# One core of Trainium2: attention and a mixture of experts in one kernel, with another order at the end of attention and the token lists' one-hots written in pairs

## The chip, the core and the metric

The kernel runs on one core of one Trainium2 chip. The core has five engines, each with its own in-order instruction queue: TensorE (PE; its weight loads are shown apart as PEld), VectorE (DVE), ScalarE (ACT), GpSimd (POOL) and SyncE (SP), which here only issues DMAs. Sixteen DMA engines serve all queues. The metric is the time of one execution on the device, in microseconds (us).

## What is computed

The input x has 8 sequences of 1024 tokens with 256 features. The reference, cut to what matters:

```python
x = x + attn(layernorm(x))        # 16 heads of 16, rotary q and kv, keys are also the values, softmax over 1024 keys
xf = layernorm(x)                 # 8192 rows of 256
x = x + ffn(xf)

def ffn(xf):
    scores = softmax(xf @ gate_w.T)              # 8 experts
    vals, idx = top_k(scores.T, 1024)            # each expert takes its 1024 best tokens
    y = layernorm(xf[idx]) * ln_w + ln_b
    h = gelu(y @ fc1.T + b1)                     # 1024 hidden units
    out = (h @ fc2.T + b2) * vals                # weighted by the score
    return xf.at[idx].add(out)                   # scattered back
```

## The kernel before

**Attention.** A group is four heads of one sequence, so 8 sequences make 32 groups. A group has 16 steps: two halves of 512 queries, and for each half eight tiles of 128 keys. In a step PE makes the scores of one key tile for two pairs of heads (`ps_s`, L587), ACT takes their exponential (`e`, L620), and every second step PE multiplies the two last tiles of `e` with the values (`ps_av`, L639). The products of two steps are copied by ACT (`avp`, L652) and added to `av` by POOL (L654); the very last add of the kernel's attention is on DVE, by the flag `end`. Beside this the row maxima of scores 13 steps ahead are taken (L536 on PE, L543 on DVE); they are over 13 steps before the end.

The order is written out by hand. A loop over steps calls the work of the step and then `run_pieces`, which advances the waiting generators by one piece each: `urgent` ones all, of `ends` the first only. A piece that yields a number waits as many steps; one that yields "x" wants a step where heavy work is let in, "y" one where light work is, and near the end every step lets both in; "d" wants a step that is even. After the loop `finish(urgent)` runs what is left there, and then the two epilogues advance in turn, one piece each, until they are done. Each engine's queue keeps the order in which its instructions were written.

When a half of a group has all its keys, `divide` turns `av` so that tokens lie on partitions (`ps_d`, L665), and divides by the sum of the exponentials (L671, L673) into `ao`. It yields 4, then "y". When the last group of a sequence has a half divided, an `epilogue` for that half of the sequence (512 tokens) is queued. Its pieces, in order:

1. fetch of the residual; 2. transposes of `ao` on PE and copies by ACT (`aoT`, L718); 3. and 4. output product for two token tiles each (`ps_o`, L725) and its add to the residual on DVE (L733); 5. to 8. the mean and variance of one token tile each on DVE (L219, L220), the last also with the reciprocal deviation on POOL (L222, L224), the normalised rows `xf` (L242), a second deviation (`again`, L232 to L236) and the add of `xf` to the residual (L739); 9. transposes of `xf` and copies (`xfT`, L767); 10. gate product (`ps_g`, L773) and its copy `lg` (L781); 11. its transpose (`ps_gt`, L784), maximum, difference `z` and exponential (L787 to L792); 12. sum, reciprocal and scores `sc` (L795 to L799); 13. nothing; 14. transpose of the scores (`ps_sc`, L804), copy `turned` (L806), and four DMAs into `by_expert` (L809).

`lg` and `turned` share one buffer (tag "lg", one of it). In the last sequence the first half's four score DMAs go alternately from the queues of SP and ACT, as the second half's do. Its `xf` and row scaling are on DVE, in earlier sequences on POOL. The write of `out` (L740) is issued in piece 8, the scaling of the rows (`rows`, L750) and their write to `rows_d` (L814) in piece 14 after the score DMAs. `rows_d` holds, for every token, its second normalisation and its eight scores; the experts gather from it. The output rows are what the experts' results are later added to.

**Choice of tokens.** A search over 30 bits finds each expert's threshold (L1009 to L1018): DVE counts the scores of `by_expert` that are not below the candidate, PE sums the counts, DVE sets the next candidate. Then each token's place in its expert's list is computed (L1027 to L1073).

**Token lists.** `token_list(e, LOW)` turns places into a list of token numbers by products of one-hot matrices. A place is split into a low and a high part (L1090, L1091, cast to bf16 at L1093). `high` (L1095) is one where the high part equals the column's number; `ids` holds `high` times the partition's number (L1103) and times the tile's number (L1104); `low` (L1129) is one where the low part equals the column's number, in chunks of 1024 columns. PE multiplies `low` and `ids` (`ps_i`, L1115), and two small DVE instructions make the index (L1142, L1144). In `high`, the second `ids` and `low`, one input is a number repeated over the whole inner row. The first list uses LOW = 64: `high` and `ids` of 1024 columns and four chunks of `low`, all of it before the experts. The other lists use LOW = 128: 512 columns and eight chunks, made in pieces beside the experts; those for experts 3 to 7 beside the second products of experts 1 to 5.

**Experts.** POOL gathers a list's rows by indirect DMA (L1152), PE transposes them (`ps_y`, L1167), DVE scales (`yT`, L1168). Expert 0 has a plain first layer (L1189), the others one with seven products in place of eight (L1230, with sums of weights on POOL at L1208 to L1211, sums of rows on DVE at L1217 to L1220). The second layer (`ps_o`, L1284) is followed by a bias add and a scaling on DVE (L1292, L1293) and an indirect DMA from POOL that adds to `out` (L1294). The next weights are loaded from SP (L959, L961).

Of the kernel before, what the change touches and what calls it, by code (L numbers as in the profile page):

```python
# [10 lines left out]
BF16 = mybir.dt.bfloat16  # L11
# [3 lines left out]
ALU = mybir.AluOpType  # L15
# [4 lines left out]
P = 128  # L20
# [7 lines left out]
def preln_attention_moe_kernel(  # L28
# [18 lines left out]
    nc = tc.nc  # L47
    B, N, D = x.shape
# [49 lines left out]
    with ExitStack() as actx:  # L98
# [531 lines left out]
        def weigh_values(i, half, chunk):  # L630

            b, g = divmod(i, NG)
            pa = ps_m.tile([P, QW], F32, tag="m", name="ps_av")
            for n, (kt, es) in enumerate(chunk):
                for h in range(4):
                    c = VS * (4 * g + h)
                    nc.tensor.matmul(  # L639
                        pa[HS * h : HS * (h + 1), :],  # L640
                        lhsT=v_bufs[b % 2][:, kt, c : c + HS],
                        rhs=es[h // 2][:, h % 2, :],
                        start=(n == 0),
                        stop=(n == len(chunk) - 1),
                    )
            if chunk[0][0] == 0:
                grp[i]["av"] = small.tile([P, QW], F32, tag="av", name="av")
                nc.scalar.copy(grp[i]["av"], pa)
            else:
                av = grp[i]["av"]  # L650
                part = small.tile([P, QW], F32, tag="avp", name="avp", bufs=3)
                nc.scalar.copy(part, pa)  # L652
                end = i == B * NG - 1 and half == 1 and chunk[-1][0] == T - 1
                (nc.vector if end else nc.gpsimd).tensor_tensor(av, av, part, ALU.add)  # L654
                if chunk[-1][0] == T - 1:
                    urgent.append(Task(divide(i, half, av)))

        def divide(i, half, av):

            b, g = divmod(i, NG)  # L660
            yield 4
            yield "y"
            pt = ps_m.tile([P, T2, 4, HS], F32, tag="m", name="ps_d")
            for t in range(T2):
                nc.tensor.transpose(  # L665
                    pt[:, t].rearrange("p h d -> p (h d)"), av[:, t * P : (t + 1) * P], ident
                )
            if b not in outs:
                outs[b] = side.tile([P, T, D], F32, tag="ao", name=f"ao_{b}")
            rden = small.tile([P, T2, 4, 1], F32, tag="rden", name="rden")  # L670
            nc.vector.reciprocal(rden, pt[:, :, :, DH : DH + 1])  # L671
            dst = outs[b][:, T2 * half : T2 * (half + 1), 4 * g * DH : 4 * (g + 1) * DH]
            nc.vector.tensor_tensor(  # L673
                dst.rearrange("p t (h d) -> p t h d", h=4),
                pt[:, :, :, 0:DH],
                rden.to_broadcast([P, T2, 4, DH]),
                ALU.mult,
            )
            finished[(i, half)] = True
# [20 lines left out]
        def residual_ahead(b, hf):  # L700
            xt = residual(b, hf)
            yield 5
            add_bias(xt)

        def epilogue(b, hf):
            ao = outs[b]
            tok = slice(hf * QW, (hf + 1) * QW)
# [32 lines left out]
            out_dma = lambda: nc.sync.dma_start(  # L740
                out[b, tok, :].rearrange("(t p) d -> p t d", p=P), xt
            )
            if last:
                out_dma()

            rows = side.tile([P, T2, ROW], F32, tag="rows", name=f"rows_{b}_{hf}")

# [58 lines left out]
            nc.scalar.copy(turned, ps[0 : T2 * E, 0:P])  # L806
            t0 = b * T + hf * T2
            for t in range(T2):
                (nc.scalar if last and t % 2 else nc.sync).dma_start(  # L809
                    by_expert[t0 // T2 :: NB, t * P : (t + 1) * P], turned[t * E : (t + 1) * E, :]  # L810
                )
            if last:
                rows_scaled()
            nc.sync.dma_start(  # L814
                rows_d[t0 * P : (t0 + T2) * P, :].rearrange("(t p) d -> p t d", p=P), rows
            )

# [166 lines left out]
    nc.gpsimd.iota(turn_i, pattern=[[1, 2], [2, KT]], base=0, channel_multiplier=0)  # L986
    turn = sel.tile([P, 2 * KT], BF16, name="turn")
    nc.gpsimd.tensor_copy(turn, turn_i.rearrange("p a c -> p (a c)"))
    part_i = sel.tile([P, 1], I32, name="part_i")
    nc.gpsimd.iota(part_i, pattern=[[0, 1]], base=0, channel_multiplier=1)  # L990
    part = sel.tile([P, 1], F32, name="part")
# [89 lines left out]
    def token_list(e, LOW, ahead=1):  # L1081
# [7 lines left out]
        halves_i = hot.tile([P, 2, NT], I32, tag="halves_i", name=f"halves_i{e}")  # L1089
        nc.vector.tensor_scalar(halves_i[:, 0], mine, LOW - 1, None, ALU.bitwise_and)  # L1090
        nc.vector.tensor_scalar(halves_i[:, 1], mine, LOW.bit_length() - 1, None, ALU.logical_shift_right)  # L1091
        split = hot.tile([P, 2, NT], BF16, tag="split", name=f"split_{e}")
        nc.vector.tensor_copy(split, halves_i)  # L1093
        high = hot.tile([P, NT, HIGH], BF16, tag=f"high{LOW}", name=f"high_{e}")
        nc.vector.tensor_tensor(  # L1095
            high,
            split[:, 1].unsqueeze(2).to_broadcast([P, NT, HIGH]),
            order.unsqueeze(1).to_broadcast([P, NT, HIGH]),
            ALU.is_equal,
        )  # L1100
        yield
        ids = hot.tile([P, NT, 2, HIGH], BF16, tag=f"ids{LOW}", name=f"ids_{e}")
        nc.vector.tensor_scalar(ids[:, :, 0, :], high, part, None, ALU.mult)  # L1103
        nc.vector.tensor_tensor(  # L1104
            ids[:, :, 1, :],
            high,
            lane[:, 0:NT].unsqueeze(2).to_broadcast([P, NT, HIGH]),
            ALU.mult,
        )
        pi = ps_i.tile([P, 2, KT], F32, tag="pi", name="ps_i")  # L1110
        def summed(c, low):
# [13 lines left out]
        for c in range(NT // CH):  # L1125
# [1 line left out]
            low = hot.tile([P, 1024], BF16, tag="low", name=f"low_{e}_{c}", bufs=4)  # L1127
            low = low.rearrange("p (c l) -> p c l", l=LOW)
            nc.vector.tensor_tensor(  # L1129
                low,  # L1130
                split[:, 0, c * CH : (c + 1) * CH].unsqueeze(2).to_broadcast([P, CH, LOW]),
                lane[:, 0:LOW].unsqueeze(1).to_broadcast([P, CH, LOW]),
                ALU.is_equal,
            )
            lows.append((c, low))
# [289 lines left out]
```

## Time and profile before

| what | us |
|---|---|
| median of three runs | 2227.04 (2224.79 to 2232.28) |
| profiled execution, its own time | 2223.82 |
| span of its instructions | 2222.1 |
| attention, to the last `ps_av` | 1655.7 |
| end of attention, to the first count of the search | 32.5 |
| search and places, to the first write of `by_token` | 50.7 |
| first list, to its index | 10.0 |
| first gather and transposes | 8.1 |
| experts, to the end | 465.0 |

The stretches add up to the span; their borders are read from the timeline, and the rest of the execution's own time, 1.7 us, lies around the span. Over the span PE is busy 92%, DVE 82%, ACT 62% and POOL 58%.

A line of the profile names a source line, an engine, an operation, and what it writes and reads (out<-in); a count and a time follow. "idle before" is the time in which the engine had nothing to run ahead of these instructions, with what ended it. "q" behind an engine means its queue: there it issues a DMA or waits. In the slices a digit is the busy share of one fortieth of the span in tenths; PEclk is the clock that TensorE was granted, in the same way.

### The profile page before, as it was taken

To read this page: it belongs to the slowest core of one execution; us is meant where nothing else is said; L and a number is where in the kernel's file an instruction comes from. 1 tells how busy PE (TensorE), PEld (TensorE's weight loads), DVE (VectorE), ACT (ScalarE), POOL (GpSimd) and SP (SyncE) were. 2 spreads that over 40 slices of the span, in tenths; PEclk is the share of its full clock that TensorE was granted. 3 is DMA by queue.
4 is the path that set the end of the run, shared out by engine and by line. 5 is a ranking of instruction groups with operands and counts; after the bars stand their busy time and mean duration, and the time that the engine had idled before them with its cause. 6 is when DMAs were issued, how large, how long until landed. Compare 5 with 4: busy or idle time off the path is not lost.

```text
span 2222.1 us, 35016 instructions
## 1 busy us (share of the span) xinstructions
PE 2054.7 (92%) x12476; PEld 1095.6 (49%) x12476; DVE 1816.0 (82%) x3443; ACT 1382.3 (62%) x1783; POOL 1292.2 (58%) x1319
## 2 busy tenths in 40 slices
PE   7999999999999999999999999999982599999998
PEld 4444544444444444444444444444441366666665
DVE  8988888998998899889889988989936667777754
ACT  2777777777887787778787777878770012222221
POOL 6667585748476765858494766724242154555542
PEclk8999999999999999999999999999995699999999
DMA  6523624632472355236225722642113033333322
GB/s 178 185 93 122 235 80 157 217 114 78 145 263 81 107 198 195 78 136 238 96 79 174 255 78 69 229 173 78 41 40 134 20 79 70 76 75 77 74 45 24
DMA packets 152702, 271.51 MB, mean 122 GB/s; under 512 B 15056, under 2 KB 67664, under 8 KB 152400
## 3 DMA queue, kind: packets, MB, share of 16 engines
q1 hardware_dynamic: 139056, 250.61, 32.9%
q0 software_dynamic: 12288, 17.05, 4.7%
q8 instruction: 98, 1.61, 0.3%
q10 hardware_dynamic: 1184, 1.62, 0.2%
q14 instruction: 76, 0.62, 0.1%
HBM read 143.93 MB, written 125.04 MB: 121 GB/s over the span
## 4 chain that ended last, share of the span: by engine, by line
PE 69%; DVE 18%; issue 5%; POOL 3%; ACT 2%; DMA 2%; SPq 0%; POOLq 0%; ACTq 0%; DVEq 0%
PE ps_av L639 20%; DVE mx L543 13%; PE ps_x L536 13%; PE ps L1230 8%; PE ps_o L1284 7%; PE ps_s L587 7%; PE ps_p L292 5%; PE ps_t L251 3%; PE ps_o L725 3%; PE ps_h L1189 1%; POOL xf L242 1%; ACT e L620 1%; DVE low L1129 1%; PE ps_d L665 1%; DVE xr L733 1%
## 5 line engine op out<-in xcount | busy, mean ns | idle before, releaser
L543 DVE TENSOR_REDUCE mx<-ps_x 128x1 f32<-128x512 f32 x2048 | 1265.0, 682 | 154.4 <-PE ps_x L536 141.1
L620 ACT ACTIVATE e<-ps_s 128x1024 f32<-128x1024 f32 x1024 | 995.3, 1025 | 87.7 <-PE ps_x L536 35.7
L536 PE MATMUL ps_x<-k,q 64*128 64x512 f32 x2048 | 719.0, 450 | 19.6 <-DVE mx L543 6.6
L587 PE MATMUL ps_s<-q,s 64*128 64x512 f32 x2048 | 622.9, 428 | 10.0 <-ACT e L620 7.1
L536 PEld LDWEIGHTS ps_x<-k,q 64*128 64x128 f32 x2048 | 348.0, 186 | 413.4 <-DVE mx L543 287.9
L639 PE MATMUL ps_av<-e,v 128*32 128x512 f32 x4096 | 492.7, 599 | 7.0 <-DVE mx L543 0.9
L654 POOL TENSOR_TENSOR av<-av,avp 128x512 f32<-128x512 f32 x191 | 243.3, 1274 | 391.7 <-ACT avp L652 375.5
L587 PEld LDWEIGHTS ps_s<-q,s 64*128 64x128 f32 x2048 | 314.3, 185 | 49.0 <-ACT e L620 31.6
L1294 POOL DMA_INDIRECT out<-o,idx x64 | 114.5, 1790 | 215.0 <-DVE o L1293 80.7
L1284 PE MATMUL ps_o<-w,hT 128*128 128x256 f32 x1024 | 230.2, 381 | 0.0
L639 PEld LDWEIGHTS ps_av<-e,v 128*32 128x32 f32 x4096 | 107.4, 109 | 241.6 <-issue 163.8
L1284 PEld LDWEIGHTS ps_o<-w,hT 128*128 128x128 f32 x1024 | 192.1, 190 | 29.0 <-issue 4.8
L652 ACT COPY avp<-ps_av 128x512 f32<-128x512 f32 x192 | 112.6, 587 | 143.8 <-PE ps_av L639 141.3
L1242 ACT COPY mid<-ps 128x512 f32<-128x512 f32 x28 | 16.0, 570 | 203.7 <-PE ps L1230 203.7
L1182 ACT ACTIVATE hT<-mid,b 128x512 f32<-128x512 f32 x112 | 77.8, 718 | 98.9 <-DVE mid L1257 73.8
L292 PE MATMUL ps_p<-wqkv,xnT 128*128 128x512 f32 (+1 forms) x288 | 130.6, 581 | 4.4 <-DVE mx L543 4.1
L1152 POOL DMA_INDIRECT g<-rows_d,idx x64 | 69.9, 1092 | 85.2 <-issue 75.5
L269 POOL TENSOR_TENSOR u<-pe,sin 128x256 f32<-128x256 f32 (+1 forms) x128 | 86.1, 693 | 54.7 <-ACT pe L263 54.7
L1292 DVE TENSOR_TENSOR o<-ps_o,b2b 128x256 f32<-128x256 f32 x64 | 27.0, 422 | 102.9 <-PE ps_o L1284 100.3
L339 POOL CAST hi<-full 128x512 fp32r<-128x512 f32 x60 | 36.8, 613 | 90.3 <-ACT full L337 81.6
L273 POOL TENSOR_TENSOR qk<-pe,u 128x512 f32<-128x512 f32 (+1 forms) x72 | 83.2, 1156 | 7.2 <-DVE pe L271 2.2
L340 POOL TENSOR_TENSOR lo<-full,hi 128x512 fp32r<-128x512 f32 x60 | 76.8, 1280 | 7.9 <-DMA s_d<-dlo 3.1
(193 smaller groups left out, 2362.6 us busy)
## 6 DMA issues: line engine op xcount, KB each, us to landing
s<-s_d SPq DMA_DIRECT2D x64, 512.0 KB
k<-k_d SPq DMA_DIRECT2D x62, 512.0 KB
q<-q_d SPq DMA_DIRECT2D x124, 256.0 KB
s_d<-dhi SPq DMA_DIRECT2D x32, 512.0 KB
s_d<-dlo SPq DMA_DIRECT2D x32, 512.0 KB
w<-in_fc_t SPq DMA_DIRECT2D x16, 1024.0 KB
q_d<-hi SPq DMA_DIRECT2D x30, 512.0 KB
q_d<-lo SPq DMA_DIRECT2D x30, 512.0 KB
```

The source lines that it names most:

```text
L269: eng.tensor_tensor(u[:, :, a * hd : (a + 1) * hd], v4[:, :, 1 - a, :], s3, ALU.mult)
L292: nc.tensor.matmul(pp, lhsT=xnT[:, kc, t % T2 * P : (t % T2 + 1) * P], rhs=w.rearrange("p a d -> p (a d)") if n == DC else w, start=(kc == 0),
L536: nc.tensor.matmul(pt, lhsT=q[r : r + 64, h // 2, j * P : (j + 1) * P], rhs=k[r : r + 64, h // 2, kh * QW : (kh + 1) * QW], start=True, st ...
L543: nc.vector.tensor_reduce(grp[i]["mx"][:, kh, h, j : j + 1], pt, AX.X, ALU.max)
L587: nc.tensor.matmul(pt[:, h % 2, :], lhsT=ones_r[r : r + 64, :] if last else k[r : r + 64, pair, kt * P : (kt + 1) * P], rhs=(top_bufs[half ...
L620: nc.scalar.activation(e.rearrange("p h q -> p (h q)"), pt.rearrange("p h q -> p (h q)"), AF.Exp, scale=DH**-0.5,)
L639: nc.tensor.matmul(pa[HS * h : HS * (h + 1), :], lhsT=v_bufs[b % 2][:, kt, c : c + HS], rhs=es[h // 2][:, h % 2, :], start=(n == 0), stop= ...
L652: nc.scalar.copy(part, pa)
L654: (nc.vector if end else nc.gpsimd).tensor_tensor(av, av, part, ALU.add)
L1230: nc.tensor.matmul(ph, lhsT=lhsT, rhs=rhs, start=True, stop=True)
L1284: nc.tensor.matmul(po, lhsT=h[:, f, j * P : (j + 1) * P], rhs=weights[e][1][:, f, :], start=(n == 0), stop=(n == FC - 1),)
L1294: nc.gpsimd.indirect_dma_start(out=out_rows[:, :], out_offset=bass.IndirectOffsetOnAxis(ap=idx[:, t : t + 1], axis=0), in_=o, in_offset=No ...
```

## The change

Two parts, with nothing else touched.

*End of attention.* In the last group `divide` yields 2 in place of 4. The last add to `av` is on DVE for both halves of the last group. The first half's four score DMAs all go through SP (`own` is true for the second half of the last sequence only). In the last sequence the write of `out`, the scaling of the rows and the write of `rows_d` leave the epilogue's middle: both halves' are kept in a list `left`, and are run at the end of the second half's epilogue, first all scalings, then for each half the write of `rows_d` and that of `out`.

*One-hots.* The parts of a place are cast to `split` with each number twice, side by side, and `lane2` holds each tile's number twice. `high`, the second `ids` and `low` are written as rows of pairs: the repeated input is read as the same pair again and again, the other as pairs of neighbours. The numbers computed are the same.

```diff
-                end = i == B * NG - 1 and half == 1 and chunk[-1][0] == T - 1
+                end = i == B * NG - 1 and chunk[-1][0] == T - 1
                 (nc.vector if end else nc.gpsimd).tensor_tensor(av, av, part, ALU.add)
...
-            yield 4
+            yield 2 if i == B * NG - 1 else 4
             yield "y"
...
+        left = []
...
-            if last:
-                out_dma()
...
-                (nc.scalar if last and t % 2 else nc.sync).dma_start(
+                (nc.scalar if own and t % 2 else nc.sync).dma_start(
                     by_expert[t0 // T2 :: NB, t * P : (t + 1) * P], turned[t * E : (t + 1) * E, :]
                 )
+            rows_out = rows_d[t0 * P : (t0 + T2) * P, :].rearrange("(t p) d -> p t d", p=P)
             if last:
-                rows_scaled()
-            nc.sync.dma_start(
-                rows_d[t0 * P : (t0 + T2) * P, :].rearrange("(t p) d -> p t d", p=P), rows
-            )
+
+                left.append((rows_scaled, rows_out, rows, out_dma))
+                if hf == 1:
+                    for scale, *_ in left:
+                        scale()
+                    for _, rows_out, rows, write in left:
+                        nc.sync.dma_start(rows_out, rows)
+                        write()
+            else:
+                nc.sync.dma_start(rows_out, rows)
...
+    lane2 = sel.tile([P, NT, 2], BF16, name="lane2")
+    nc.gpsimd.tensor_copy(lane2, lane[:, 0:NT].unsqueeze(2).to_broadcast([P, NT, 2]))
...
-        split = hot.tile([P, 2, NT], BF16, tag="split", name=f"split_{e}")
-        nc.vector.tensor_copy(split, halves_i)
+        split = hot.tile([P, 2, NT, 2], BF16, tag="split", name=f"split_{e}")
+        nc.vector.tensor_copy(split, halves_i.unsqueeze(3).to_broadcast([P, 2, NT, 2]))
+
+        def in_pairs(t):
+            return t.rearrange("p t (l a) -> p t l a", a=2)
+
+        def each(two, n):
+
+            return two.unsqueeze(2).to_broadcast([P, two.shape[1], n // 2, 2])
+
+        def rows_of(numbers, tiles):
+
+            two = numbers.rearrange("p (l a) -> p l a", a=2).unsqueeze(1)
+            return two.to_broadcast([P, tiles, two.shape[2], 2])
...
         nc.vector.tensor_tensor(
-            high,
-            split[:, 1].unsqueeze(2).to_broadcast([P, NT, HIGH]),
-            order.unsqueeze(1).to_broadcast([P, NT, HIGH]),
-            ALU.is_equal,
+            in_pairs(high), each(split[:, 1], HIGH), rows_of(order, NT), ALU.is_equal
         )
...
-            ids[:, :, 1, :],
-            high,
-            lane[:, 0:NT].unsqueeze(2).to_broadcast([P, NT, HIGH]),
-            ALU.mult,
+            in_pairs(ids[:, :, 1, :]), in_pairs(high), each(lane2, HIGH), ALU.mult
         )
...
             nc.vector.tensor_tensor(
-                low,
-                split[:, 0, c * CH : (c + 1) * CH].unsqueeze(2).to_broadcast([P, CH, LOW]),
-                lane[:, 0:LOW].unsqueeze(1).to_broadcast([P, CH, LOW]),
+                in_pairs(low),
+                each(split[:, 0, c * CH : (c + 1) * CH], LOW),
+                rows_of(lane[:, 0:LOW], CH),
                 ALU.is_equal,
             )
```

## The prediction

> **What bounds the kernel now.** I read the page's slices first: they show where TensorE is not full.
>
> ```profile
> PE   7999999999999999999999999999982599999998
> PEclk8999999999999999999999999999995699999999
> ```
>
> Only slices 30 to 32 (1667 to 1833 us) fall, work and granted clock together. Busy time by stretch says which parts of the kernel these are:
>
> ```profile
> 1655.70:1688.20 32.50, 17.15 (x98) 11.43 (x97) 16.86 (x49) 5.50 (x13) 11.11 (x16) 0.74 0.26 88
> 1738.90:1748.90 10.00, 4.10 (x128) 3.73 (x128) 8.51 (x13) 0.00 (x0) 0.00 (x0) 0.50 0.01 2
> 1757.00:2222.00 465.00, 448.46 (x2053) 305.68 (x2051) 314.37 (x497) 102.84 (x156) 219.60 (x151) 0.99 0.31 63
> ```
>
> Columns: stretch, length, busy time of PE, PEld, DVE, ACT, POOL, clock, DMA. The end of attention (32.5 us) is a chain of small steps through all engines; the first token list (10 us) is DVE's, 8.51 busy; the experts are PE's. The change touches these three. The chain of waits for the first ends so:
>
> ```profile
> 1680.06 1.43 ACTq L809
> 1681.52 3.24 DMA by_expert<-turned
> ...
> 1684.90 0.26 ACT turned L806
> ...
> 1685.81 2.33 DMA by_expert<-turned
> ```
>
> The timeline gives the hand-offs around it:
>
> ```profile
> 1655.64 2.00 PE L725 MATMUL ps_o<-wo,aoT 128*128 128x256 f32 x8
> 1674.73 1.38 DVE L242 TENSOR_SCALAR xf<-xr,mv_b,rs_b 128x256 f32<-128x256 f32 x4 [1.47 <-POOL rs_b L224]
> 1682.22 0.23 ACT L792 ACTIVATE z<-z 128x32 f32<-128x32 f32 x1 [2.18 <-DMA by_expert<-turned]
> 1684.90 0.25 ACT L806 COPY turned<-ps_sc 32x128 f32<-32x128 f32 x1 [2.46 <-DMA by_expert<-turned]
> 1688.20 0.75 DVE L1009 TENSOR_SCALAR_CACHE_REDUCE ge<-by_expert,cand 128x512 uint8<-128x512 f32 x1 [4.04 <-DMA by_expert<-turned]
> ```
>
> The second half's exp (z, input ready 1680.20) waits 2.0 us while ACT issues two of the first half's score DMAs; its `turned` (scores in PSUM at 1683.62) waits 1.25 us for those DMAs to release the one buffer.
>
> For the lists I read the waits of PE from 1800 to 2110, then the shapes of DVE's groups after 1740:
>
> ```profile
> PE ps_i L1115 <- DVE low L1129: 6.5, 5, 1.3
> L1129 DVE TENSOR_TENSOR low<-split,lane 128x1024 bf16<-128x1024 bf16 x60 | 77.5, 1307 | 3.1 <-PE ps_i L1115 3.1
> L1095 DVE TENSOR_TENSOR high<-split,turn 128x1024 bf16<-128x1024 bf16 x1 | 1.2, 1227 | 0.1
> L1217 DVE TENSOR_TENSOR ysum<-yT,yT 128x512 f32<-128x512 f32 x7 | 4.7, 675 | 0.0
> L1103 DVE TENSOR_SCALAR ids<-high,part 128x1024 bf16<-128x1024 bf16 x1 | 0.5, 485 | 0.1
> ```
>
> PE waits for the lists five times, 1.3 us each, once for each of experts 1 to 5, and for nothing else there.
>
> **End of attention, part by part.** A step of the loop is one key tile, 2.45 us near the end. With "divide" two steps on, the first half's ps_d moves from step 13 to 11 of the last group, its transposes from 15 to 13, its two ps_o groups from step 16 and after to steps 14 and 15. The av add of that half goes from POOL (1.31 us, behind 4.74 us of bias adds) to an idle DVE (0.69): free, since ps_d at step 11 waits for neither. ps_d (0.66) and the transposes (1.09) lie beside ACT's exps. The two aoT copies (1.10 on ACT) delay the exps of step 14; PE is then in ps_av and does not notice.
>
> The ps_o groups do cost: the first, 2.0 us, stands in PE's queue between ps_av (ends 1652.05) and the last scores, so these go from 1651.98 to about 1653.9; behind them the second (1.9) ends at 1656.45, and only then the last ps_av (1.95) can run: it ends at about 1658.4 instead of 1655.71, **2.7 us late**.
>
> From there on the order is new, each half advancing one piece in turn with the first now two ahead. After the last ps_av: copy, add, ps_d, reciprocal, ao, 3.1. DVE then does the first half's three remaining statistics (3 x 0.54), POOL its rstd (1.35), DVE xf (1.38), to +7.6; the transposes of xf sit in PE's queue ahead of the second half's last ps_o, which so ends at +10.3 to 10.9. The first half's gate product, logits and softmax interleave with the second half's four statistics: last one at +14.5 to 15.6, rstd, xf starts +16.0 to 17.1. Before, xf started 19.0 after ps_av (1674.73). From xf to the issue of the scores 7.15: the row distance 1674.73 to 1679.78, where lm starts, and 2.1 of softmax, transpose and copy. The 2.0 on ACT's queue is gone with the first half's four DMAs all on SP, and so is the 1.25: those start at about +15.3, take four issues of 0.62 on SP and land by +20.4, before the second half's lg wants the same buffer at +20.2 to 21.3. Issue to the first count 3.0 as now (1685.18 to 1688.20). Sum +26.1 to 27.2 against 32.5: 5.9 less, with the 2.7: **-3.1 us**. Bounds: -5.1, if the loop absorbs half of the ps_o, to +0.5, if it takes 1.1 more and lg waits 1 for the buffer, with some rounding.
>
> Moved: eight row scalings of 0.35 (2.8 us on DVE) now come after both halves' softmax, under the DMA wait of 4.04 (uncovered they would cost 2.8); the first half's no longer meet POOL's 2.46 us add (that stretch took 3.23). Two rows_d and two out writes (2.1 MB) stand on SP behind the last scores and ahead of the weights. First reader: the gather at 1749.8, 60 us later; weights wanted at 1758. Four more issues of 0.4 on SP and some 6 us of transfer at the 350 GB/s seen here: nothing on the path. If that cover went, 6 us.
>
> **The lists.** Equal pairs let both inputs of the one-hots step through neighbouring 16-bit elements. No two-input bf16 row with such steps exists in the trace. Ends: no gain (1.22 us for 1024), and the one-input bf16 row, 0.485. That row takes as long as the 512 f32 one-input at L1053 (0.479), so 16-bit elements pass at double rate; two-input f32 of 512 takes 0.675 to 0.69 (L1217). I take **0.69 for 1024**, 0.43 for 512. The cast of `split` writes 256 instead of 128: 0.23 to at most 0.36, I take +0.1. lane2 is one small POOL copy (near 0.29, as L983) in its idle 57.8 us.
>
> First list, serial: high -0.53, second ids -0.53, first low -0.53; then PE's four groups run without the three waits of 0.2 between them, -0.6, since PE needs 0.93 for a group and DVE 0.6 instead of 1.13; cast +0.1. **-2.1** (bounds +0.1 and -2.7).
>
> Five later waits: in each, DVE's queue is without a gap from 1916.8 to the low that PE wants (ends 1930.87; PE had been free 1.34). Three lows lie in it: 3 x 0.53 = 1.59 saved, some 0.1 lost waiting for a ps_o. 1.34 goes with 0.15 to spare; I count 1.2 of each, **-6.0** (bounds 0 and -6.5). The margin is thin because one low of each list runs 2.29 beside POOL's weight sums, which this does not change: 1.07 of it is POOL's.
>
> By the Trainium skill, GPSIMD Engine Reference, section "1. Specifications", POOL shares its SBUF interfaces with VectorE, and instructions with two SBUF inputs contend for them; pairs leave two inputs, so by that rule the collision stays (rival B), and the 2.29 agrees. By VectorE: DVE Perf Modes, section "The perf-mode tier table", two-input bf16 runs at twice the rate with unit steps: an estimate of 0.69 for 1024, by which the sum would stay; no run here shows it yet.
>
> **Sum.** -3.1 - 2.1 - 6.0 = -11.2. The profiled execution took 2223.8, giving 2212.6; it lies 3.2 under the median of 2227.0, so I forecast 2227.0 - 11.2 = **2215.8**.
>
> **Rivals.**
> (A) Pairs pass no faster. Inner runs of two are the shortest in the program; nothing shows them fast. Attention alone, -3.1, and 0.1 for each of six casts on the path, +0.6: 2224.5.
> (B) POOL's port eats the margin: lows that come earlier meet two of POOL's four weight sums. For it: 2.29, and POOL's 2.34 instead of 1.27 at 1919.1. One more collision, 1.07, leaves about 1.0 of each wait: -3.1 - 2.1 - 1.8 = -7.0: 2220.0.
> (D) The end of attention gains nothing: ps_o in the loop and the buffer cost what the order wins (+0.5): 2219.4.
> (C) Slower: short inner rows cost DVE more than single steps. L1073, which writes scattered rows, goes from 270 ns for 64 elements to 941 for 448: 1.75 ns each instead of 1.04. A low would be 1.95, +0.73: six in the first list +4.4, three for each of five waits +11: -3.1 + 4.5 + 11 = +12.4: 2239.4. It turns the total from a low of 1.37 (21 x 0.15 = 3.1). Against it: L1073 reads PSUM and its strides are wide; here the output is dense.
>
> **How the numbers follow.** Forecast 0.55, A 0.13, B 0.12, D 0.10, C 0.10. Range 2209 (every bound at its best from the median is 2212.7, less the 3.2 of the profiled execution) to 2226 (A and a spread of 1.6); it leaves out C and tails of the others, under 2 in 10. A measurement here tells 0.3%, 6.7 us, from no change. Faster: 0.54 + half of B + 0.06 of D = 0.66; same: A's 0.12, the rest of B and D, 0.23; slower 0.11.
>
> **What would show it.** low at 0.69 and no PE wait at L1115 after 1800; the first list from `split` to the index 2.1 shorter; the last ps_av up to 2.7 later relative to the loop, then the first count 26 to 27 after it; no ACT score issue in the first half. Wrong if low stays at 1.2 or above, or if ps_av's delay exceeds 5.

## The result, and the profile after

| | before | after |
|---|---|---|
| median, us | 2227.04 (2224.59 to 2232.28, 5 runs) | 2212.03 (2210.21 to 2215.76, 5 runs) |
| profiled execution, its own time | 2223.82 | 2212.03 |
| its span | 2222.1 | 2210.2 |

The ratio of the times is 0.9936, with a 95% interval of 0.9924 to 0.9948: the changed kernel is 15.0 us faster by the medians and 11.8 by the two profiled executions.

The slices of the page of the changed kernel, in the places of those shown of before:

```profile
PE   7999999999999999999999999999993499999998
PEclk9999999999999999999999999999996699999999
```

The dip is where it was and reads 9, 3 and 4 where there were 8, 2 and 5; no slice outside it fell, so no new gap opened. Busy time by stretch says more (columns as before: stretch, length, PE, PEld, DVE, ACT, POOL, clock, DMA):

```profile
1659.20:1686.60 27.40, 12.55 (x84) 7.76 (x81) 13.36 (x48) 5.51 (x13) 10.98 (x16) 0.77 0.21 71
1737.40:1744.80 7.40, 3.59 (x128) 3.49 (x128) 5.14 (x13) 0.00 (x0) 0.00 (x0) 0.50 0.01 2
1817.00:2148.60 331.60, 331.60 (x1523) 227.60 (x1522) 213.92 (x394) 78.12 (x120) 154.93 (x119) 1.00 0.34 73
```

The end of attention is 27.4 us instead of 32.5; the first list takes DVE 5.14 of work instead of 8.51 (0.27 of which was the place write just ahead of it). The third row covers experts 1 to 6: PE is busy in all of it. The same stretch before, from the first product with seven terms to the last expert's first:

```profile
1821.30:2160.30 339.00, 332.46 (x1522) 227.56 (x1522) 249.88 (x394) 78.41 (x120) 172.87 (x120) 1.00 0.34 72
```

There 6.5 us of PE were idle. The 0.86 more of busy time goes with the five waits, 0.17 each: it is there again in attn_only and one_side, which keep the waits, and in no kernel without them. I take it for the price of starting PE again. From the borders of all stretches, read from the two timelines, comes this account:

| stretch | before | after | difference | foreseen |
|---|---|---|---|---|
| start to the fifth last `ps_av` | 1635.30 | 1636.13 | +0.8 | 0 |
| from there to the end of the last `ps_av` | 20.41 | 23.10 | +2.7 | +2.7 |
| to the first count of the search | 32.49 | 27.37 | -5.1 | -5.9 |
| search and places, to `split`'s inputs | 51.06 | 50.88 | -0.2 | 0 |
| first list, to its index | 9.64 | 7.26 | -2.4 | -2.1 |
| to the first product with seven terms | 72.44 | 72.38 | -0.1 | 0 |
| experts 1 to 6 | 338.89 | 331.48 | -7.4 | -6.0 |
| the rest | 61.84 | 61.64 | -0.2 | 0 |

The first row is no work of the change: over all the kernels here, none of which changes what runs ahead of it, this border lies between 1634.7 and 1639.3. So much does one execution differ from another before the change begins, and that is why what follows goes by stretches and not by the times of single runs. The other rows add up to -12.7, where the foreseen ones make -11.3 (-11.2 with the prediction's rounding).

The chain of waits of the changed kernel, at the end of attention:

```profile
1681.56 0.27 ACT turned L806
1681.85 1.41 ACTq L809
1683.26 0.03 issue
1683.29 2.99 DMA by_expert<-turned
...
1686.60 0.77 DVE ge L1019 x2
```

And its timeline, with the loop's end first:

```profile
1652.80 1.99 PE L727 MATMUL ps_o<-wo,aoT 128*128 128x256 f32 x8
1655.32 1.94 ACT L620 ACTIVATE e<-ps_s 128x1024 f32<-128x1024 f32 x2 [1.56 <-PE ps_s L587]
1655.38 1.99 PE L727 MATMUL ps_o<-wo,aoT 128*128 128x256 f32 x8
1657.31 1.92 PE L639 MATMUL ps_av<-e,v 128*32 128x512 f32 x16
...
1672.81 2.41 SPq L809 DMA_DIRECT2D by_expert<-turned  x4
1674.58 1.38 DVE L242 TENSOR_SCALAR xf<-xr,mv_b,rs_b 128x256 f32<-128x256 f32 x4 [1.47 <-POOL rs_b L224]
1680.07 0.23 ACT L792 ACTIVATE z<-z 128x32 f32<-128x32 f32 x1 [1.02 <-DVE z L789]
1681.56 0.26 ACT L806 COPY turned<-ps_sc 32x128 f32<-32x128 f32 x1 [1.27 <-PE ps_sc L804]
1686.60 0.75 DVE L1019 TENSOR_SCALAR_CACHE_REDUCE ge<-by_expert,cand 128x512 uint8<-128x512 f32 x1 [3.54 <-DMA by_expert<-turned]
```

The reader is to see three things. The two output-product groups of the first half stand in PE's queue, 1.99 each: one before the last scores, so that ACT waits 1.56 us for these, and one between them and the last `ps_av`, which comes 2.7 us late. The exponential `z` and the copy `turned` now wait for their own inputs (1.02 and 1.27), no longer for score DMAs (2.18 and 2.46 before). But of the second half's scores the first that ACT issues takes 1.41 us at ACT's queue, the step from there to the landing takes 2.99, and the count starts 4.75 after `turned` was ready to go, not 3.0.

The lists, by the shapes of DVE's groups after 1725 us:

```profile
L1148 DVE TENSOR_TENSOR low<-split,lane 128x1024 bf16<-128x1024 bf16 x60 | 40.4, 685 | 10.5 <-PE ps_i L1134 7.9 <-issue 1.3 <-PE ps_h L1208 1.3
L1120 DVE TENSOR_TENSOR high<-split,lane 128x512 bf16<-128x512 bf16 x7 | 3.0, 426 | 0.2
L1105 DVE CAST split<-halves_i 128x256 bf16<-128x256 int32 x8 | 2.4, 294 | 0.3
L1120 DVE TENSOR_TENSOR high<-split,turn 128x1024 bf16<-128x1024 bf16 x1 | 0.7, 691 | 0.1
```

and by the waits of PE after 1740 us:

```profile
PE ps_i L1134 <- DVE low L1148: 3.7, 1, 3.7
```

One `low` takes 685 ns where it took 1307. The one wait that is left is the start of the first list; after 1800 us there is none, where there were five of 1.3.

### The profile page after: what moved, and what is told of

The parts are those of the page before. It is cut to its first block, busy times and chain, and to the rows that moved or that the text cites. A ratio compares the mean times of both kernels' runs of the same rounds, so it can differ in the third digit from the quotient of the medians.

```text
span 2210.2 us, 35017 instructions
## 1 busy us (share of the span) xinstructions
PE 2053.9 (93%) x12476; PEld 1093.1 (49%) x12476; DVE 1765.1 (80%) x3444; ACT 1382.7 (63%) x1783; POOL 1271.0 (58%) x1319
## 4 chain that ended last, share of the span: by engine, by line
PE 72%; DVE 16%; issue 4%; POOL 3%; DMA 3%; ACT 2%; SPq 0%; POOLq 0%; ACTq 0%; DVEq 0%
PE ps_av L639 21%; DVE mx L543 13%; PE ps_x L536 13%; PE ps_o L1303 10%; PE ps L1249 8%; PE ps_s L587 7%; PE ps_p L292 5%; PE ps_t L251 3%; PE ps_o L727 3%; PE ps_h L1208 1%; POOL xf L242 1%; ACT e L620 1%; DMA top_d<-mrows 1%; PE ps_d L665 1%; PE ps_y L1186 1%
## 5 line engine op out<-in xcount | busy, mean ns | idle before, releaser
L1313 POOL DMA_INDIRECT out<-o,idx x64 | 102.2, 1597 | 208.9 <-DVE o L1312 85.2
L1171 POOL DMA_INDIRECT g<-rows_d,idx x64 | 63.7, 995 | 98.7 <-issue 69.2
```

What stands on the lines that cost most here:

```text
L1313: nc.gpsimd.indirect_dma_start(out=out_rows[:, :], out_offset=bass.IndirectOffsetOnAxis(ap=idx[:, t : t + 1], axis=0), in_=o, in_offset=No ...
```

## The experiments

Each kernel is the changed one with the edit shown, unless the text says otherwise. Stretches in us from each kernel's own profiled execution; "loop" is from the fifth last `ps_av` to the end of the last, "tail" from there to the first count, "list" and "experts" as in the account above.

| kernel | loop | tail | both | list | experts |
|---|---|---|---|---|---|
| before | 20.41 | 32.49 | 52.9 | 9.64 | 338.9 |
| after | 23.10 | 27.37 | 50.5 | 7.26 | 331.5 |
| attn_only | 23.10 | 27.38 | 50.5 | 9.65 | 338.9 |
| lists_only | 20.40 | 32.33 | 52.7 | 7.26 | 331.5 |
| wait_four | 22.04 | 34.65 | 56.7 | 7.26 | 331.5 |
| two_queues | 23.10 | 25.57 | 48.7 | 7.27 | 331.5 |
| low_only | 23.12 | 27.35 | 50.5 | 8.33 | 331.5 |
| one_side | 24.71 | 27.36 | 52.1 | 8.64 | 338.8 |
| rows_early | 23.12 | 32.36 | 55.5 | 7.26 | 331.5 |
| later_products | 21.48 | 28.44 | 49.9 | 7.26 | 331.5 |
| two_queues_timed | 23.11 | 25.59 | 48.7 | 7.26 | 331.5 |
| changed_again | 23.10 | 27.38 | 50.5 | 7.27 | 331.5 |
| act_earlier | 24.12 | 25.62 | 49.7 | 7.26 | 331.5 |
| out_late | 23.10 | 27.48 | 50.6 | 7.27 | 331.5 |

**Each part by itself.** attn_only is the changed end of attention with the lists of before.

> The edits at the end of attention alone, the lists as before. Theory (the two parts add): against before the span falls by about 2.5 us: the last ps_av ends 2.7 later in the loop, and from its end to the first count of the search it takes 27.4 instead of 32.5. Rival: the attention edits give nothing by themselves, and all of the measured gain is the lists': the span stays within 1 us of before.

lists_only is the other half: the end of attention of before with the lists in pairs.

> The one-hots in pairs alone, the end of attention as before. Theory: low takes 0.69 us instead of 1.22, the first list from its first split to its index 7.26 instead of 9.65, no wait of PE for low after 1800 us, 7.4 less for experts 1 to 5: about 9.8 us off the span, ratio near 0.9956. Rival: part of the 7.4 comes from the changed start of the experts (transfers at the end of attention moved): then less than 8.5 us.

Measured: attn_only 2221.84 (2220.23 to 2226.82, 10 runs) against 2226.12 for the kernel before, ratio 0.9983 (0.9974 to 0.9993). lists_only 2216.72 (2215.76 to 2218.26, 5 runs), ratio 0.9961 (0.9947 to 0.9976). The product of the two is 0.9944, inside the whole change's interval, and in the table each part moves its own stretches alone. So the parts add, and the lists are the larger: 9.8 us of their stretches against 2.4 of the end of attention.

**The end of attention, its division as late as before.**

```diff
-            yield 2 if i == B * NG - 1 else 4
+            yield 4
```

> The changed kernel with divide yielding 4 again in the last group, all else as changed. Theory (the order makes the one queue pay): the last ps_av comes 2.7 earlier in the loop, but the second half's copy of its scores again waits for the first half's score DMAs to free the one buffer, and the first ACT issue of a score DMA costs its 1.4 in the second half: from the last ps_av to the first count 32 to 33 us as before, in all 2.5 to 3.5 us slower than the changed kernel. Rival (the queue alone does it): the exp's wait of 2.0 and the buffer's 1.25 vanish without the earlier divide: 29 to 30 us, and the kernel is 0.5 to 1 us faster than the changed one.

Measured: 2219.72 in one run; both stretches 56.7. That is 3.8 more than before the change, and more than was expected. ACT's timeline shows where:

```profile
1682.07 0.25 ACT L806 COPY turned<-ps_sc 32x128 f32<-32x128 f32 x1 [0.57 <-PE ps_gt L784]
1687.38 0.25 ACT L806 COPY turned<-ps_sc 32x128 f32<-32x128 f32 x1 [4.63 <-DMA by_expert<-turned]
```

With the halves close together again, the second `turned` waits 4.63 us for the first half's four DMAs to release the one buffer. These leave one after the other from SP, and here a load of weights (1 MB) has left ahead of them:

```profile
1681.22 0.38 SPq L966 DMA_DIRECT2D w<-in_fc_t  x1
1682.35 2.42 SPq L809 DMA_DIRECT2D by_expert<-turned  x4
```

From 1682.3 to 1685.2 the DMA engines moved 0.97 MB in packets of over 2 KB. A row of the scores has 512 bytes, so none of the scores was among it: they moved behind the weights. In the changed kernel the first half's scores leave at 1672.81, six us ahead of that load (1678.77). The single queue is bearable there because the earlier division draws the halves apart and brings the scores ahead of the weights; what each is worth wasn't told apart. Some 1.5 of the loop's 22.04 is a single `ps_av` that took 3.44 instead of 1.92 in this execution; what stretched it stays open.

**Both queues for the first half's scores, as before the change, the rest as changed.**

```diff
-                (nc.scalar if own and t % 2 else nc.sync).dma_start(
+                (nc.scalar if last and t % 2 else nc.sync).dma_start(
```

> The changed kernel with the first half's score DMAs again alternating between SP and ACT. Theory (the first issue from ACT after a long pause is the dear one, 1.41 us, and in the new order ACT is idle when the first half issues): it is paid there, the second half's two ACT issues take 0.6 each, and from issue to the first count it takes 3.0 instead of 4.8: 25.6 from the last ps_av to the first count, 1.7 us better than the changed kernel. Rival 1: the issue holds up ACT as it did before, so the second half's copies come later and nothing is won. Rival 2: 1.4 is paid after every pause, so that the second half pays again: 27.4.

Measured: 2209.17 in one run; the tail 25.57, 1.8 shorter than with one queue. ACT's timeline, both halves:

```profile
1671.12 0.26 ACT L806 COPY turned<-ps_sc 32x128 f32<-32x128 f32 x1 [1.30 <-PE ps_sc L804]
1671.40 2.05 ACTq L809 DMA_DIRECT2D by_expert<-turned  x2
...
1680.39 1.35 ACTq L809 DMA_DIRECT2D by_expert<-turned  x2
```

The first half's two issues take 2.05 us, 1.42 of it the first, in a place where ACT has nothing to do; the second half's take 0.57 and 0.75, and the first count comes 3.00 after they begin (1680.39 to 1683.39). In the changed kernel it is the second half that pays the long first issue, and there everything waits for it. The chain of waits of two_queues shows that this is only half of the difference:

```profile
1680.39 0.57 ACTq L809
...
1680.99 2.09 DMA by_expert<-turned
```

The issue is 0.84 shorter (0.57 for 1.41), and the step behind it, from ACT's second issue to the landing, 0.90 (2.09 for 2.99). What differs there is the order of the issues. SP goes on to the second half's scores and then to the write of `rows_d` (528 KB) without waiting for ACT. In the changed kernel that write is issued ahead of ACT's second score DMA (1683.29), with two queues behind it (1680.99). SP's queue in the one and in the other:

```profile
1683.15 0.40 SPq L820 DMA_DIRECT2D rows_d<-rows  x1
```

```profile
1681.69 0.41 SPq L820 DMA_DIRECT2D rows_d<-rows  x1
```

From 1683.6 to 1685.6 the DMA engines of the changed kernel move 0.53 MB of SP's queue and nothing of ACT's, so the last score DMA, whose issue ended at 1683.90, moves only after that. The first half of two_queues has the long issue without such a write beside it, and there ACT's second DMA has moved by 1674.3, 0.85 after its issue ended at 1673.45. No run holds the write back by itself, so this second half of the loss is read from the traces and not tested alone. The step "one queue for the first half", which the prediction took for a gain, is a loss of 1.8 us in the order that the change makes.

**Which of the one-hots count.** low_only keeps `low` in pairs and has `high` and the second `ids` in the old form:

```diff
-            in_pairs(high), each(split[:, 1], HIGH), rows_of(order, NT), ALU.is_equal
+            high,
+            split[:, 1, :, 0:1].to_broadcast([P, NT, HIGH]),
+            order.unsqueeze(1).to_broadcast([P, NT, HIGH]),
+            ALU.is_equal,
...
-            in_pairs(ids[:, :, 1, :]), in_pairs(high), each(lane2, HIGH), ALU.mult
+            ids[:, :, 1, :],
+            high,
+            lane[:, 0:NT].unsqueeze(2).to_broadcast([P, NT, HIGH]),
+            ALU.mult,
```

> The changed kernel with pairs in low alone; high and the second ids as before. Theory (in the experts only the three lows of the gapless stretch of DVE matter): no wait of PE for low after 1800, 331.5 us from the first seven-product layer to that of expert 7, as in the changed kernel; the first list, which is serial, gives back two times 0.53: 8.3 us instead of 7.26. Rival: high and ids are part of the backlog, so the five waits come back in part, 1.5 us or more in sum.

Measured: 2213.93 in one run; the first list 8.33 instead of 7.26, so 1.07 for two instructions of 1024, 0.53 each; the experts 331.5, with no wait of PE. Beside the experts the two cost nothing either way.

**Whether it is the pair that counts, or the output written in neighbours.** one_side writes `low` in pairs, but reads the repeated input as one number again and again:

```diff
-                each(split[:, 0, c * CH : (c + 1) * CH], LOW),
+                split[:, 0, c * CH : (c + 1) * CH, 0:1]
+                .unsqueeze(3)
+                .to_broadcast([P, CH, LOW // 2, 2]),
```

> The changed kernel with low still written in pairs, but its repeated input read as one number again and again (inner step 0) instead of as a pair. Theory (both inputs have to step through neighbouring 16-bit elements): low takes 1.22 us again, the five waits of PE are back with about 6.5 us, the experts take 338.9, the first list about 8.6. Rival: the dense output or the other input's step does it: low stays at 0.69 and the span stays that of the changed kernel.

Measured: 2224.90 in one run. Its waits of PE after 1800 us and its group of `low`:

```profile
PE ps_i L1134 <- DVE low L1148: 6.5, 5, 1.3
```

```profile
L1148 DVE TENSOR_TENSOR low<-split,lane 128x1024 bf16<-128x1024 bf16 x60 | 77.5, 1304 | 4.6 <-PE ps_i L1134 4.6
```

Both lines are those of before the change again (1304 ns a piece for 1307, the same 6.5 us in five waits). The fast form needs both inputs to step through neighbours; the repeated one standing still is enough to lose all of it. By the Trainium skill, Vector Engine (DVE) Microarchitecture Reference, section "5.1 Performance modes — why throughput varies by op and dtype", one element read again and again as an input of a two-source operation on 2-byte operands runs at the plain rate, while a row read again and again gets the double one; 1.22 (a `low` that meets nothing on POOL) and 0.685 (where the row is a pair) agree. The 1.6 more of this kernel's loop is again a pause of one execution: its code there is the changed kernel's.

**The moved writes.** rows_early has the `out` write, the scaling and the write of `rows_d` back in each half's epilogue:

```diff
+            if last:
+                out_dma()
...
-                left.append((rows_scaled, rows_out, rows, out_dma))
-                if hf == 1:
-                    for scale, *_ in left:
-                        scale()
-                    for _, rows_out, rows, write in left:
-                        nc.sync.dma_start(rows_out, rows)
-                        write()
-            else:
-                nc.sync.dma_start(rows_out, rows)
+                rows_scaled()
+            nc.sync.dma_start(rows_out, rows)
```

> The changed kernel with the scaling of the rows and the two writes back at their old places (out in piece 8, rows_d behind the score DMAs of each half). Theory (both are hidden, this part of the change is worth nothing): from the start of step 8's product to the first count within 0.5 us of the changed kernel's 50.5. Rival: the transfers ahead of the second half's scores make them land later, or the scaling beside POOL's add holds up the logits: 1 to 2.4 us more.

Measured: 2220.45 in one run; the tail 32.36, 5.0 more, against the expectation that this would be hidden. The queue of SP:

```profile
1672.10 10.01 SPq L742 DMA_DIRECT2D out<-xr  x2
1682.20 2.58 SPq L812 DMA_DIRECT2D by_expert<-turned  x4
```

and ACT beside it:

```profile
1675.02 0.25 ACT L809 COPY turned<-ps_sc 32x128 f32<-32x128 f32 x1 [1.30 <-PE ps_sc L807]
1686.05 0.27 ACT L784 COPY lg<-ps_g 128x128 f32<-128x128 f32 x1 [5.60 <-DMA by_expert<-turned]
```

Both `out` writes stand in SP's queue ahead of the first half's scores, and the second of them waits for POOL's last add to the residual, which ends at 1681.7 here. The scores, ready at 1675.3, stand behind it until 1682.2; the next `lg` wants their buffer and waits 5.60. Before the change the two writes stood in the same places, but there the add ended at 1679.1 and the scores were ready only at 1680.0. Counted from the last `ps_av`, the new order brings the scores 10.8 us forward and the add only 3.4, so that a place in the queue that had cost nothing came to cost 5 us. out_late tells the `out` write from the scaling and `rows_d`: only the two `out` writes are kept for the end.

```diff
-                left.append((rows_scaled, rows_out, rows, out_dma))
+                left.append(out_dma)
+                rows_scaled()
...
+            if last and hf == 1:
+                for write in left:
+                    write()
```

> The changed kernel with the scaling of the rows and the write of rows_d back behind each half's score DMAs, as in rows_early, but the two writes of out kept for the end. Theory (in rows_early it was the second half's write of out, waiting on SP for POOL's add, that held the first half's score DMAs behind it): 50.5 us from the start of step 8's product to the first count, as in the changed kernel, not the 55.5 of rows_early. Rival (the row scaling or the rows_d transfers were the cause): 53 to 55.5 again.

Measured: 2213.08 in one run; both stretches 50.6, as in the changed kernel. Its queue of SP:

```profile
1672.83 2.41 SPq L809 DMA_DIRECT2D by_expert<-turned  x4
1677.09 0.36 SPq L817 DMA_DIRECT2D rows_d<-rows  x1
...
1681.87 1.21 SPq L809 DMA_DIRECT2D by_expert<-turned  x2
...
1683.61 1.60 SPq L742 DMA_DIRECT2D out<-xr  x2
```

The write of `rows_d` between the two halves' scores hurts nobody. Of all that was moved, the two `out` writes alone carry the 5 us.

**Can the 2.7 us of the loop be had back?** later_products has both queues, holds the first half's output products back by a step, and gives its `turned` a buffer of its own:

```diff
+            if last and hf == 0:
+                yield 1
             for t2 in range(T2 // 2):
                 yield "x"
...
-            turned = small.tile([T2 * E, P], F32, tag="lg", name="turned", bufs=1)
+            turned = small.tile([T2 * E, P], F32, tag="tail" if last and hf == 0 else "lg", name="turned", bufs=1)
```

> The kernel two_queues with the first half's output products one step later (a wait of one step ahead of them) and a buffer of its own for the first half's scores. Theory (the first output product between ps_av and the last scores is what makes the loop end later): the last ps_av 1.5 us earlier, 21.6 instead of 23.1 after step 8's product, and 25.6 to 26.2 from there to the first count: about 1 us better than two_queues. Rival: with the first half one piece less ahead its statistics meet the second half's, and the time from the last ps_av grows by as much or more.

Measured: 2213.35 in one run. The loop is 21.48, so 1.6 came back, but the tail grows to 28.44 against 25.57 with both queues:

```profile
1679.41 2.06 ACTq L811 DMA_DIRECT2D by_expert<-turned  x2
1681.51 0.27 ACT L783 COPY lg<-ps_g 128x128 f32<-128x128 f32 x1 [2.13 <-issue]
```

The first half now reaches its scores when the second half's `lg` is due, and ACT's long issue stands ahead of it: `lg` comes 2.28 after the end of the last `xfT` copy, against 0.77 in two_queues. That is 1.5 of the 2.9 by which the tail grew; the other 1.4 were lost before, where the second half's normalised rows `xf` start 16.7 after the last `ps_av` and not 15.4. The sum, 49.9, is 1.2 worse than that of two_queues.

**One queue or two, in time.**

> two_queues once more, timed beside the changed kernel on one chip. Theory: 25.6 us from the last ps_av to the first count, 1.8 less than the changed kernel, ratio to before near 0.9930. Rival: the first look's shorter span came from elsewhere (its loop also began earlier) and the median is that of the changed kernel.

> The changed kernel itself, timed beside two_queues on one chip: 27.4 us from the last ps_av to the first count, median 1.8 us above two_queues, ratio to before near 0.994.

Measured on one chip, with the kernel before at 2227.01: two_queues_timed 2212.29 (2208.07 to 2216.35, 6 runs), ratio 0.9935 (0.9921 to 0.9950); changed_again, which is the changed kernel, 2213.62 (2212.36 to 2215.19, 5 runs), ratio 0.9938 (0.9925 to 0.9951). By time the two are not told apart. By the tail they are: 25.57 and 25.59 against 27.37 and 27.38, two executions each. A faster version than the changed kernel is thus shown for this stretch, and not for the whole time.

**Is it the first issue from ACT that is long?** act_earlier lets the sequence before the last issue one of its score DMAs from ACT, some 41 us ahead:

```diff
-                (nc.scalar if own and t % 2 else nc.sync).dma_start(
+                (nc.scalar if own and t % 2 or b == B - 2 and hf == 1 and t == 3 else nc.sync).dma_start(
```

> The changed kernel with one of the four score DMAs of the sequence before the last (second half) issued from ACT, some 41 us ahead of the last ones. Theory (only a pause of hundreds of us makes ACT's first issue dear): the early issue takes 1.4, the last two 0.6, and the time from the last ps_av to the first count falls from 27.4 to about 25.6. Rival (41 us are enough to make it dear again): 1.4 both times and 27.4.

Measured: 2212.01 in one run. ACT's queue:

```profile
1640.52 1.47 ACTq L809 DMA_DIRECT2D by_expert<-turned  x1
...
1682.63 1.35 ACTq L809 DMA_DIRECT2D by_expert<-turned  x2
```

The early one takes 1.47 alone, the two later ones 1.35 together (0.58 and 0.74), and the tail is 25.62. So the long issue is the first of these, wherever it stands; two loads that ACT issues at the start of the kernel (0.50 and 0.53) don't spare it. Whether the long pause since those makes it long, or that it is the first of its form, isn't told apart. The two later ones also come ahead of the write of `rows_d` again (1683.24 against 1683.93). In the loop the early issue is no bargain: it stands between ACT's exponentials, and the loop is 1.0 longer (24.12).

## Why the prediction held, and where it did not

Forecast were 2215.8 and 11.2 us less; measured were 2212.0 and 15.0 by the medians, 11.8 by the profiled executions. The sum was thus near against the profiled execution that it was made from, but that it is so near is in part luck. By the account of the stretches the lists gained 9.8 for 8.1 foreseen, the end of attention 2.4 for 3.1, and the stretches that were to stay as they are 0.5; the 0.8 lost before the change begins hides what is over. The forecast's shift by 3.2 to the median of three shows up as the difference between 11.8 and 15.0: before, the profiled execution lay 3.2 under the median, after, at the median itself. No stretch holds these 3.2; they are the spread of single executions.

**The lists: mechanism right, size small.** 0.69 and 0.43 us were taken for the one-hots, 0.685 and 0.426 came, and the cast of `split` rose by less than the 0.1 allowed (0.294). The estimate by the Trainium skill, VectorE: DVE Perf Modes, section "The perf-mode tier table (the rule you actually need)", was 0.69 and is borne out. The first list gained 2.4 for 2.1: `high` and the second `ids` gave 1.07 by low_only, as assumed. The term that was too small is the five waits, "I count 1.2 of each, **-6.0**": all of each 1.3 went, and with it the 0.17 of PE's busy time, which the prediction did not count, so 7.4.

The margin was counted as 0.15 because of one sentence, "one low of each list runs 2.29 beside POOL's weight sums, which this does not change". It did change. The timelines of POOL and DVE before, for expert 2:

```profile
1919.08 2.34 POOL L1209 TENSOR_TENSOR wsum<-wsum,w 128x512 f32<-128x512 f32 x1
1919.09 1.21 DVE L1129 TENSOR_TENSOR low<-split,lane 128x1024 bf16<-128x1024 bf16 x1
1922.62 1.31 POOL L1211 TENSOR_TENSOR wsum<-w,wsum 128x512 f32<-128x512 f32 x1
1922.73 2.29 DVE L1129 TENSOR_TENSOR low<-split,lane 128x1024 bf16<-128x1024 bf16 x1
```

and after:

```profile
1911.94 1.82 POOL L1228 TENSOR_TENSOR wsum<-wsum,w 128x512 f32<-128x512 f32 x1
1911.95 0.68 DVE L1148 TENSOR_TENSOR low<-split,lane 128x1024 bf16<-128x1024 bf16 x1
...
1914.95 1.26 POOL L1230 TENSOR_TENSOR wsum<-w,wsum 128x512 f32<-128x512 f32 x1
1916.36 0.73 DVE L1148 TENSOR_TENSOR low<-split,lane 128x1024 bf16<-128x1024 bf16 x1
```

Before, two lows of each list met a weight sum. Where both began within 0.01 us, POOL paid (2.34 for 1.27); where POOL was 0.11 ahead, DVE did (2.29 for 1.22). The first meeting stays, at a smaller price for POOL (1.82). With shorter work on both sides POOL's sums are through at 1916.2, and the second low starts at 1916.36: nothing is left to meet. The same holds in all five lists. Rival B, which let the lows meet two sums, falls for that reason, A and C by the 685 ns.

**The end of attention: one term right, one wrong.** The 2.7 us that the first half's `ps_o` puts into the loop came as worked out. From the last `ps_av` on, `xf` of the second half started +15.4 after it, a little ahead of the +16.0 to 17.1 foreseen, and 7.26 from there to the scores' issue were foreseen as 7.15. Then the step that failed: "Issue to the first count 3.0 as now (1685.18 to 1688.20)". It measured 4.75. The 3.0 was the price of the second half's issue behind a first half that had already used ACT's queue: the page before showed that first use, 1.43 at `ACTq`, in the very chain that the prediction quotes. The prediction priced the removal of those two issues as a gain of 2.0 and not what they leave to the next one: 0.84 for the issue itself and, by the traces, 0.90 because ACT's second issue then falls behind the write of `rows_d`. The same order stood in the first half before the change, where the chain that the prediction quotes has 3.24 for the landing: `rows_d` was issued at 1681.37, ACT's second score DMA at 1681.52. The prediction read that wait as the price of two queues. So the stretch gained 5.1 for 5.9, though what lies ahead of the issue came a microsecond better; both together 2.4 for 3.1. two_queues, which keeps the other edits, gives 3.00 from issue to count and 4.2 for both.

Rival D, no gain here, is refuted by attn_only, if narrowly: its interval ends at 0.9993.

**What was worked out as free.** The `av` add on DVE took 1.50 and not 0.69, and began at 1638.87 while POOL's bias adds ran on to 1639.81; it was free all the same. The scalings lie in DVE's wait for the scores, 2.19 us at 1680.87. Of the four writes behind the last scores the first, of `rows_d`, was not free: it moved ahead of ACT's late second score DMA (the 0.90 above). It had stood behind the scores before the change too, but there both of ACT's issues had ended by 1686.37, ahead of it (1686.49). And "nothing on the path" was an answer to half of the question. It priced the writes in their new place, and not what the old place would cost under the new order; rows_early and out_late show that the move of the `out` writes is what keeps 5 us off the end of attention.

Open stay what makes ACT's first issue long, and what makes PE pause some 1.5 us in single executions. That the four score DMAs of the second half might all go through SP, past ACT's queue, wasn't tried, nor was a later write of `rows_d`.

## What to carry to other kernels

When an operation is taken off the path, ask whether it also paid something once for those behind it, as a queue's first issue does, and who pays it then; the long item in the chain is not always the fault of its place. When work is brought forward, look at what stands ahead of it in each in-order queue: a write that waits for its producer holds back all that is behind it, also where that had cost nothing in the old order. Look also at which large transfer is issued just ahead of a small one that the path waits for, from whichever queue. And look for a repeated input in 16-bit one-hots and masks on VectorE: stored twice and read as pairs, it made these instructions 1.8 times as fast for one cast of double length.

## What the runs showed of the hardware

- The first score DMA that ACT issues, 1640 to 1690 us after its last issue, takes 1.41 to 1.47 us; the next ones take 0.57 to 0.75, even 41 us later. SP, which issues all through the kernel, takes 0.56 to 0.65 for the same in the changed kernel.
- A small DMA issued behind a large one can wait for it, from its own queue or another. A 4 KB score DMA of ACT's queue stood still until 1.7 us after its issue had ended, while 0.53 MB of SP's queue moved; one with no such write beside it had moved 0.85 us after. Four score DMAs of SP's queue stood behind 0.97 MB of weights.
- Two bf16 inputs read in rows of only two elements take 0.685 us for 1024 columns and 0.426 for 512; two f32 inputs take 0.675 for 512. With one input standing still 1024 take 1.22.
- DVE and POOL instructions with two inputs each seem to take turns rather than share: a `low` that came 0.11 us after a weight sum took 1.07 longer for 1.2 of overlap, and where the two began within 0.01 us the sum took 1.08 longer beside a `low` of 1.21 and 0.55 beside one of 0.68.
